# The first layer's token lists: small products over four token tiles at a time, with unlike tiles masked

## The chip, the cores and the metric

The kernel runs on one core of one Trainium2 chip. Its time is the device time of one execution in microseconds; the median of the runs is compared. A core has five engines that are told of here by these names: PE (TensorE, matrix products; PEld is its loading of weights), DVE (VectorE), ACT (ScalarE), POOL (GpSimd) and SP (SyncE, which issues most of the DMA transfers).

## The reference

Two layers work on `x` (8 x 256 tokens of 256 values), each with an attention and a feed-forward part. The change lies in the feed-forward part of the first layer. Its tokens are dealt out to 8 experts of 256 tokens each, one expert after the other, and each expert takes the 256 best of those that are left:

```python
def balanced_assignment(scores):            # T = 2048 tokens, E = 8 experts
    C = T // E
    taken = jnp.zeros((T,), dtype=bool)
    parts = []
    for e in range(E):
        s = jnp.where(taken, -jnp.inf, scores[:, e])
        _, idx = jax.lax.top_k(s, C)
        parts.append(idx)
        taken = taken.at[idx].set(True)
    return jnp.concatenate(parts)
...
sort_by_expert = balanced_assignment(scores)
routed = feat[sort_by_expert].reshape(E, C, D)
h = layer_norm(routed, ln_g, ln_b)
h = jax.nn.gelu(jnp.einsum('ecd,edf->ecf', h, w1) + b1[:, None, :])
h = jnp.einsum('ecf,efd->ecd', h, w2) + b2[:, None, :]
out = routed + h                            # put back at the tokens' own places
```

The order of the tokens inside an expert's list does not matter, since each row is put back where it came from.

## The kernel before, in words

**Order.** The order of the instructions on each engine is written out by hand (the part runs under a manual schedule); each engine works through its own queue in that order. `work` is a queue of small pieces of TensorE work with a cost each, mostly 0.43 us: two products with 128x256 f32 results. `fill(us)` (L1179) takes pieces from it until their costs reach the number given. The pieces are first the keys and values of the second layer's attention (`keys`, `vals`, lines L1398 and L1422), later each expert's two matrix products (`up`, L2388, and `down`, L2405).

**Search.** For each of the first seven experts `search` (L2158) finds the score above which the expert's 256 tokens lie, in five rounds. A round counts on VectorE how many scores of each row lie above a threshold (`count`, L2172), sums the counts by a small product on TensorE (`pcn`, L2189, waits for the count), and makes the next threshold on VectorE (L2194, L2199). Between a count and its product the fillers run: 1.29 us of them a round for experts 0, 1 and 2, around 1.73 to 2.58 for the later ones.

**Lists.** `list_tokens` (L2216) turns the threshold into the list of the expert's tokens, in steps. For experts 0 and 1 all steps run between two searches, with fillers between; for experts 2 to 5 one step is put into each round of the next search; the last two lists run side by side after the last search, with 1.29 us of fillers between steps. The 2048 tokens stand as 16 tiles of 128. The steps are:

1. `sel` marks the chosen tokens (L2227, L2231), and `pse` (L2236) turns the marks into columns.
2. `ppl` (L2262, L2263) gives each token its place in the list; a token that is not chosen gets a place out of range. `place` splits into `place >> 4` and `place & 15`. `oab` (L2270) holds the two as one-hot rows of 16 in f16, and `ob` (L2274) is the second one times the token's number.
3. `pid` (L2278): for each of the 16 tiles, a 128x16 block of `oab` (the weights) times the 128x16 block of `ob`, all summed in one 16x16 block of PSUM. The entry (a, b) is the number of the token at place 16a + b. `ids16` (L2282) is its copy in f16.
4. `pix` (L2286): two products with the constant `rowsel` spread the 16 rows over 128 partitions, so that partition p of half r holds row (128r + p) // 16. `m` (L2290) masks away all but column p mod 16 with `bsel`, `idf` (L2292) sums what is left, and `ids` (L2294) holds the numbers as integers.
5. POOL gathers the rows of the list from DRAM by two indirect transfers (L2297) into `R`, and `hand_over` puts the expert up for its products.

**After the list.** `ffn` (L2332) puts two more pieces into `work`: `norm_rows` (ACT, L2342, waits for the gathered rows) and `turn_rows` (TensorE transposes `prt`, L2369, then ACT writes `RT`, L2373), and then the expert's products. `Y` (L2414) is scattered to DRAM by POOL (L2415). The weights of expert e + 2 are loaded (`load_later`, by SP) once those of expert e are used up.

**Set-up.** `rowsel` is built on POOL between 24 and 27 us (L1649 to L1662): a fill, two selects that leave a band, and a cast to f16. POOL's next result is the root for `cs` (L1751), which is first read at `bnd` (L1862).

Of the kernel before, what the change touches and what calls it, by code (L numbers as in the profile page):

```python
# [9 lines left out]
F32 = mybir.dt.float32  # L10
# [4 lines left out]
ALU = mybir.AluOpType  # L15
# [4 lines left out]
P = 128  # L20
# [1066 lines left out]
def fast_path(  # L1087
# [33 lines left out]
    nc = tc.nc  # L1121
    B, S, D = x.shape
    T = B * S
    NT = T // P
# [6 lines left out]
    NCT = CAP // P  # L1131
# [7 lines left out]
    F16 = mybir.dt.float16  # L1139
# [121 lines left out]
    pr = l0.enter_context(tc.tile_pool(name="pr", bufs=1))  # L1261
    pm = l0.enter_context(tc.tile_pool(name="pm", bufs=2))
    ac = l0.enter_context(ExitStack())
    pa = ac.enter_context(tc.tile_pool(name="pa", bufs=1))
    acp = l0.enter_context(ExitStack())
    ps_t = acp.enter_context(tc.tile_pool(name="ps_t", bufs=4, space=PSUM))
# [30 lines left out]
    for dst, src, i in (  # L1297
# [12 lines left out]
        out=bqd.rearrange("o (b c) -> (o b) c", b=B),  # L1310
        in_=L0_xattn_bq.partition_broadcast(B),
    )
    nc.scalar.dma_start(
        out=WZ[:, :, DH : 2 * DH],
        in_=L0_xattn_Wq.rearrange("(kc p) c -> p kc c", p=P),
# [181 lines left out]
    bsel = pr.tile([P, NCT, 16], F32, name="bsel")  # L1497
# [88 lines left out]
    for h in range(TPB):  # L1586
# [4 lines left out]
            start=True,  # L1591
            stop=True,
# [11 lines left out]
        pattern=[[1, 32]],  # L1604
        base=1,
        channel_multiplier=0,
# [16 lines left out]
        out=tri,  # L1623
        in_=tri,
        pattern=[[1, P]],
        compare_op=ALU.is_gt,
        fill=0.0,
        base=0,
        channel_multiplier=-1,
    )  # L1630

    iab = pr.tile([P, NT, 2, 16], I32, name="iab")
    for j, base in enumerate((BASE // 16, 0)):
        nc.gpsimd.iota(
            iab[:, :, j, :],
            pattern=[[0, NT], [1, 16]],
            base=base,
            channel_multiplier=0,
        )
    tok = pr.tile([P, NT, 16], F16, name="tok")  # L1640
    nc.gpsimd.iota(
        tok,
        pattern=[[P, NT], [0, 16]],
        base=0,
        channel_multiplier=1,
        allow_small_or_imprecise_dtypes=True,
    )

    rows_f = pa.tile([16, NCT, P], F32, name="rows_f")  # L1649
    nc.gpsimd.memset(rows_f, 1.0)  # L1650
    for sign, base in ((1, 1), (-1, 16)):
        nc.gpsimd.affine_select(
            out=rows_f,
            in_=rows_f,
            pattern=[[sign * P, NCT], [sign, P]],
            compare_op=ALU.is_gt,
            fill=0.0,
            base=base,
            channel_multiplier=-sign * 16,
        )  # L1660
    rowsel = pr.tile([16, NCT, P], F16, name="rowsel")
    nc.gpsimd.tensor_copy(rowsel, rows_f)  # L1662
    cc.close()

    for kc in range(KC):
# [10 lines left out]
    for tt in range(2):  # L1676
# [4 lines left out]
            start=True,  # L1681
# [534 lines left out]
    def list_tokens(e, then):  # L2216

        if e == E - 1:

            sel = pm.tile([P, TB], BF16, tag="sel", name="sel")  # L2220
            nc.vector.tensor_scalar(
                sel, taken[e - 1], -1.0, 1.0, ALU.mult, ALU.add
            )
        else:
            n, thr = low[e]
            taken.append(pm.tile([P, TB], BF16, tag="taken", name="taken"))
            nc.vector.tensor_scalar(taken[e], n, thr, None, ALU.is_gt)  # L2227
            sel = taken[e]
            if e:
                sel = pm.tile([P, TB], BF16, tag="sel", name="sel")  # L2230
                nc.vector.tensor_tensor(sel, taken[e], taken[e - 1], ALU.subtract)  # L2231
        yield

        pse = ps_t.tile([P, 4, 4], F32, tag="pt", name="pse")
        for j in range(4):
            nc.tensor.matmul(  # L2236
                pse[:, j, :], sel[:, j * P : (j + 1) * P], first, start=True, stop=True
            )
        selt = pm.tile([P, NT], BF16, tag="selt", name="selt")
        nc.vector.tensor_scalar(  # L2240
            selt.rearrange("p (g j) -> p j g", j=4),
            pse,
            1.0,
            None,
            ALU.mult,
            ALU.add,
            accum_out=cnts[:, e : e + 1],
        )
        before = pm.tile([P, NT], BF16, tag="before", name="before")
        nc.vector.memset(before[:, 0:1], 0.0)  # L2250
        nc.vector.tensor_tensor_scan(
            before[:, 1:],
            onesb[:, 0 : NT - 1],
            selt[:, 0 : NT - 1],
            0.0,
            ALU.mult,
            ALU.add,
        )
        yield

        ppl = ps_t.tile([P, NT], F32, tag="pt", name="ppl")
        nc.tensor.matmul(ppl, tri, selt, start=True, stop=False)  # L2262
        nc.tensor.matmul(ppl, onesb, before, start=False, stop=True)  # L2263
        place = pm.tile([P, NT], I32, tag="place", name="place")
        nc.vector.tensor_copy(place, ppl)
        ab = pm.tile([P, NT, 2], I32, tag="ab", name="ab")
        nc.vector.tensor_scalar(ab[:, :, 0], place, 4, None, ALU.logical_shift_right)
        nc.vector.tensor_scalar(ab[:, :, 1], place, 15, None, ALU.bitwise_and)
        oab = pm.tile([P, NT, 2, 16], F16, tag="oab", name="oab")
        nc.vector.tensor_tensor(  # L2270
            oab, ab.unsqueeze(3).to_broadcast([P, NT, 2, 16]), iab, ALU.is_equal
        )
        ob = pm.tile([P, NT, 16], F16, tag="ob", name="ob")
        nc.vector.tensor_tensor(ob, oab[:, :, 1, :], tok, ALU.mult)  # L2274
        yield
        pid = ps_t.tile([16, 16], F32, tag="pt", name="pid")
        for c in range(NT):
            nc.tensor.matmul(  # L2278
                pid, oab[:, c, 0, :], ob[:, c, :], start=(c == 0), stop=(c == NT - 1)
            )  # L2280
        ids16 = pm.tile([16, 16], F16, tag="ids16", name="ids16")
        nc.vector.tensor_copy(ids16, pid)  # L2282
        yield
        pix = ps_t.tile([P, NCT, 16], F32, tag="pt", name="pix")
        for r in range(NCT):
            nc.tensor.matmul(  # L2286
                pix[:, r, :], rowsel[:, r, :], ids16, start=True, stop=True
            )
        m = pm.tile([P, NCT, 16], F32, tag="m", name="m")
        nc.vector.tensor_tensor(m, pix, bsel, ALU.mult)  # L2290
        idf = pm.tile([P, NCT], F32, tag="idf", name="idf")
        nc.vector.tensor_reduce(idf, m, AX.X, ALU.add)  # L2292
        ids = pm.tile([P, NCT], U32, tag="ids", name="ids", bufs=4)
        nc.vector.tensor_copy(ids, idf)  # L2294
        R = pf.tile([P, NCT, D + 2], F32, tag="R", name="R")
        for r in range(NCT):
            nc.gpsimd.indirect_dma_start(  # L2297
                out=R[:, r, :],
                out_offset=None,
                in_=NMd,  # L2300
                in_offset=bass.IndirectOffsetOnAxis(ap=ids[:, r : r + 1], axis=0),
            )
        then(e, ids, R)
        if e == E - 1:
            for r in range(NCT):
                nc.vector.tensor_scalar(
                    at0[:, r, :], row0, idf[:, r : r + 1], None, ALU.is_equal
                )
# [974 lines left out]
    class Up(Unit):  # L3283
        n = TB
# [733 lines left out]
```

## Time and profile before

| | |
|---|---|
| median of 3 runs | 796.91 us (796.48 to 799.59) |
| the profiled execution | 797.35 us |
| its span | 795.6 us |
| granted TensorE clock, mean | 0.995 |
| DMA over the span | 110.88 MB, mean 139 GB/s |

The span runs from the first to the last recorded instruction of the profiled execution; the remaining 1.75 us lie around it. A row of a timeline gives start, length, engine, line, operation, output and inputs with their shapes, and in square brackets how long the engine stood idle before and what ended it. Rows of like instructions in a row are merged ("x16"): the length then runs from the start of the first to the end of the last. Ends of products are modelled, so that two products of 0.17 us may start 0.03 us apart. A row of a tile gives count, the shortest, middle and longest duration in ns, and when the first and last started.

### The profile page before, as it was taken

How to read it: one execution, taken by the hardware profiler on the slowest of the kernel's cores; microseconds unless marked ns; L12 is line 12 of the kernel's file. 1: busy time of each engine (PE TensorE's matmuls, PEld its weight loads, DVE VectorE, ACT ScalarE, POOL GpSimd, SP SyncE). 2: the span in 40 equal slices, each digit the busy share in tenths (PEclk: the TensorE clock that was granted, in tenths of full speed). 3: DMA queues.
4: the chain of work that ended last, by engine and by line, in shares of the span. 5: the costliest groups of instructions: out<-in, count | busy, mean ns of one | idle time of the engine just before them, and what ended most of it. 6: DMA issues, size and time to landing. Idle time of an engine off the chain costs nothing. (4 is left out here: it accounts for less than half of the span.)

```text
span 795.6 us, 13571 instructions
## 1 busy us (share of the span) xinstructions
PE 778.4 (98%) x5008; PEld 617.2 (78%) x5008; DVE 523.1 (66%) x1477; ACT 367.3 (46%) x678; POOL 218.8 (28%) x293
## 2 busy tenths in 40 slices
PE   7999999999999989999999999999999999999997
PEld 6547778888755544548898988898989899999986
DVE  6367887650377886556948595758575959686732
ACT  3334455333378987331416354535353545443330
POOL 6334123131126646533330001111122311203030
PEclk9999999999999999999999999999999999999999
DMA  8294666498261111251114676797659554311023
GB/s 265 74 310 79 223 198 188 160 284 240 71 182 34 28 28 41 65 189 69 42 46 111 197 228 199 173 318 200 190 117 314 104 185 115 98 14 21 8 28 136
DMA packets 110163, 110.88 MB, mean 139 GB/s; under 512 B 31848, under 2 KB 100680, under 8 KB 110056
## 3 DMA queue, kind: packets, MB, share of 16 engines
q1 hardware_dynamic: 101416, 96.61, 40.8%
q0 software_dynamic: 7920, 13.02, 7.9%
q8 instruction: 41, 0.67, 0.4%
q10 hardware_dynamic: 752, 0.30, 0.1%
q14 instruction: 34, 0.28, 0.1%
HBM read 80.61 MB, written 25.37 MB: 133 GB/s over the span
## 5 line engine op out<-in xcount | busy, mean ns | idle before, releaser
L3609 POOL DMA_INDIRECT Od<-Y,ids x32 | 53.2, 1662 | 279.0 <-DVE Y L3421 163.9
L3281 ACT COPY B<-a 128x512 f32<-128x512 f32 (+1 forms) x54 | 28.7, 531 | 166.8 <-PE a L3293 110.4
L2679 ACT ACTIVATE ex<-p,scale 128x1024 f32<-128x1024 f32 x64 | 67.7, 1111 | 16.8 <-PE p L2671 16.8
L3293 PE MATMUL a<-T,HP 128*128 128x256 f32 x288 | 73.9, 379 | 0.0
L3293 PE MATMUL a<-RT,wab 128*128 128x256 f32 x256 | 66.3, 381 | 0.0
L3143 DVE TENSOR_TENSOR cc<-e,s 128x512 f32<-128x512 f32 x44 | 30.4, 690 | 54.1 <-PE e L3293 54.1
L3143 DVE TENSOR_TENSOR act<-act 128x256 f32<-128x256 f32 (+1 forms) x120 | 61.4, 512 | 2.7
L2388 PE MATMUL ph<-RT,w 128*128 128x256 f32 x256 | 62.0, 390 | 0.0
L2405 PE MATMUL py<-w,A 128*128 128x256 f32 x256 | 61.6, 387 | 0.0
L3293 PEld LDWEIGHTS a<-T,HP 128*128 128x128 f32 x288 | 54.0, 190 | 7.0
L3293 PEld LDWEIGHTS a<-RT,wab 128*128 128x128 f32 x256 | 46.6, 190 | 7.3 <-issue 1.6
L2388 PEld LDWEIGHTS ph<-RT,w 128*128 128x128 f32 x256 | 45.1, 190 | 8.0 <-ACT RT L2373 0.5
L2928 POOL DMA_INDIRECT Td<-HP,to x32 | 33.8, 1056 | 62.7 <-DMA Td<-HP,to 55.3
L2405 PEld LDWEIGHTS py<-w,A 128*128 128x128 f32 x256 | 46.3, 190 | 6.1
L2397 ACT ACTIVATE A<-ph,b1c 128x256 f32<-128x256 f32 x64 | 30.3, 473 | 43.8 <-PE ph L2388 39.6
L3143 DVE TENSOR_TENSOR act<-act,cc 128x512 f32<-128x512 f32 x44 | 30.3, 689 | 13.6 <-ACT act L3327 13.3
L2671 PE MATMUL p<-QM,KT 32*128 32x512 f32 x256 | 37.9, 644 | 1.1 <-ACT ex L2679 0.8
L2415 POOL DMA_INDIRECT Yd<-Y,ids x16 | 15.8, 987 | 75.7 <-DVE Y L2414 22.5
L3308 ACT COPY s<-a 128x512 f32<-128x512 f32 x44 | 25.8, 585 | 20.0 <-PE a L3293 20.0
L2688 PE MATMUL pv<-ex,VA 128*32 128x256 f32 x512 | 32.2, 394 | 2.3 <-DVE run L2902 1.5
L3293 PE MATMUL B<-RT,wab 128*128 128x256 f32 x128 | 32.9, 379 | 0.0
L3293 PE MATMUL e<-RT,HP 128*128 128x256 f32 x128 | 32.8, 379 | 0.0
(526 smaller groups left out, 1712.0 us busy)
## 6 DMA issues: line engine op xcount, KB each, us to landing
w<-in_L_ffn_w_dram SPq DMA_DIRECT2D x16, 1024.0 KB, 6.4
wab<-in_L_ffn_w_e_dram SPq DMA_DIRECT2D x16, 1024.0 KB, 8.6
wc<-in_L_ffn_w_e_dram SPq DMA_DIRECT2D x8, 1024.0 KB
sab<-in_L_ffn_w_e_dram SPq DMA_DIRECT2D x32, 256.0 KB, 5.8
R<-Td SPq DMA_DIRECT2D x8, 530.0 KB, 8.2
sc<-in_L_ffn_w_e_dram SPq DMA_DIRECT2D x16, 256.0 KB, 4.2
Td<-blank SPq DMA_DIRECT2D x2, 1590.0 KB
X<-in_x_dram SPq DMA_DIRECT2D x4, 512.0 KB
```

Of the source, the lines that this page charges most:

```text
L2388: nc.tensor.matmul(ph, w1[:, kc, f * P : (f + 1) * P], RT[:, kc, :], start=(kc == 0), stop=(kc == KC - 1),)
L2397: nc.scalar.activation(A[:, f, :], ph, AF.Gelu_apprx_tanh, bias=b1c[:, e, f : f + 1])
L2405: nc.tensor.matmul(py, A[:, f, r * P : (r + 1) * P], w2[:, f, :], start=(f == 0), stop=(f == NF - 1),)
L2671: nc.tensor.matmul(ps[g // 2][:, g % 2].rearrange("p m q -> p (m q)"), KT[rows, c, k0 : k0 + P], QM[b][rows, c].rearrange("p m q -> p (m q)"),
L2679: nc.scalar.activation(e4[:, 2 * j : 2 * j + 2], ps[j], AF.Exp, scale=scale)
L2688: nc.tensor.matmul(pvs[b, c][32 * g : 32 * g + 32, m, :], VA[:, b * TPB + kt, 8 * c + 2 * g + m, :], ex[b, c, kt][:, g, m, :], start=(kt = ...
L2928: nc.gpsimd.indirect_dma_start(out=Td, out_offset=bass.IndirectOffsetOnAxis(ap=to[g][:, k, j : j + 1], axis=0), in_=HP[:, GT * g + j, :], ...
L3143: eng.tensor_tensor(out, a, b, op)
L3281: nc.scalar.copy(self.b[:, 0 : self.n], self.a[:, 0 : self.n])
L3293: nc.tensor.matmul(ps[:, m * HT2 : (m + 1) * HT2], self.w.get(m, left, self.k), self.x.part[right], start=start and m == 0, stop=True, ski ...
L3308: nc.scalar.copy(self.s2, self.a)
L3609: nc.gpsimd.indirect_dma_start(out=Od, out_offset=bass.IndirectOffsetOnAxis(ap=ids, axis=0), in_=Y, in_offset=None, compute_op=ALU.add,)
```

## The change

Four token tiles are taken together (`BL = 4`). The one-hot block of four tiles is a weight of 128x64, and `ob` of the same four tiles a moving operand of 128x64, so that `pid` becomes 64x64 and needs four products in place of sixteen. Of its 4 x 4 blocks of 16x16 only those on the diagonal pair a tile with itself; the copy to `ids16` becomes a product with the mask `like`, which is 1 on the diagonal blocks and 0 elsewhere. The four diagonal blocks are not yet added up: `rowsel` gets 64 rows, so that `pix` adds the four rows that belong to one place group, and leaves 64 columns; `m` is four times as wide, and the sum `idf` runs over all 64 columns. `oab` is laid out with the two one-hot rows apart (2, tiles, 16), so that four tiles lie side by side. `rowsel` and `like` are built once on POOL at the start.

```diff
-    rows_f = pa.tile([16, NCT, P], F32, name="rows_f")
-    nc.gpsimd.memset(rows_f, 1.0)
-    for sign, base in ((1, 1), (-1, 16)):
+    BL = 4
+    rows_f = pa.tile([16 * BL, 16, NCT * P // 16], F32, name="rows_f")
+    nc.gpsimd.memset(rows_f, 0.0)
+    for i in range(BL):
         nc.gpsimd.affine_select(
             out=rows_f,
             in_=rows_f,
-            pattern=[[sign * P, NCT], [sign, P]],
-            compare_op=ALU.is_gt,
+            pattern=[[-1, 16], [0, NCT * P // 16]],
+            compare_op=ALU.not_equal,
+            fill=1.0,
+            base=-16 * i,
+            channel_multiplier=1,
+        )
+    rowsel = pr.tile([16 * BL, NCT, P], F16, name="rowsel")
+    nc.gpsimd.tensor_copy(
+        rowsel.rearrange("a r p -> a (r p)"), rows_f.rearrange("a n b -> a (n b)")
+    )
+    like = pr.tile([16 * BL, BL, 16], F32, name="like")
+    nc.gpsimd.memset(like, 1.0)
+    for sign, base in ((1, 0), (-1, 15)):
+        nc.gpsimd.affine_select(
+            out=like,
+            in_=like,
+            pattern=[[-16 * sign, BL], [0, 16]],
+            compare_op=ALU.is_ge,
             fill=0.0,
             base=base,
-            channel_multiplier=-sign * 16,
-        )
-    rowsel = pr.tile([16, NCT, P], F16, name="rowsel")
-    nc.gpsimd.tensor_copy(rowsel, rows_f)
+            channel_multiplier=sign,
+        )
...
-        oab = pm.tile([P, NT, 2, 16], F16, tag="oab", name="oab")
+        oab = pm.tile([P, 2, NT, 16], F16, tag="oab", name="oab")
         nc.vector.tensor_tensor(
-            oab, ab.unsqueeze(3).to_broadcast([P, NT, 2, 16]), iab, ALU.is_equal
+            oab,
+            ab.rearrange("p n t -> p t n").unsqueeze(3).to_broadcast([P, 2, NT, 16]),
+            iab.rearrange("p n t w -> p t n w"),
+            ALU.is_equal,
         )
         ob = pm.tile([P, NT, 16], F16, tag="ob", name="ob")
-        nc.vector.tensor_tensor(ob, oab[:, :, 1, :], tok, ALU.mult)
+        nc.vector.tensor_tensor(ob, oab[:, 1], tok, ALU.mult)
         yield
-        pid = ps_t.tile([16, 16], F32, tag="pt", name="pid")
-        for c in range(NT):
+        pid = ps_t.tile([16 * BL, 16 * BL], F32, tag="pt", name="pid")
+        for c in range(0, NT, BL):
             nc.tensor.matmul(
-                pid, oab[:, c, 0, :], ob[:, c, :], start=(c == 0), stop=(c == NT - 1)
-            )
-        ids16 = pm.tile([16, 16], F16, tag="ids16", name="ids16")
-        nc.vector.tensor_copy(ids16, pid)
+                pid,
+                oab[:, 0, c : c + BL, :].rearrange("p n w -> p (n w)"),
+                ob[:, c : c + BL, :].rearrange("p n w -> p (n w)"),
+                start=(c == 0),
+                stop=(c == NT - BL),
+            )
+        ids16 = pm.tile([16 * BL, 16 * BL], F16, tag="ids16", name="ids16")
+        nc.vector.tensor_tensor(
+            ids16, pid, like.rearrange("a n w -> a (n w)"), ALU.mult
+        )
         yield
-        pix = ps_t.tile([P, NCT, 16], F32, tag="pt", name="pix")
+        pix = ps_t.tile([P, NCT, 16 * BL], F32, tag="pt", name="pix")
         for r in range(NCT):
             nc.tensor.matmul(
                 pix[:, r, :], rowsel[:, r, :], ids16, start=True, stop=True
             )
-        m = pm.tile([P, NCT, 16], F32, tag="m", name="m")
-        nc.vector.tensor_tensor(m, pix, bsel, ALU.mult)
+        m = pm.tile([P, NCT, 16 * BL], F32, tag="m", name="m")
+        nc.vector.tensor_tensor(
+            m.rearrange("p r (n w) -> p (r n) w", w=16),
+            pix.rearrange("p r (n w) -> p (r n) w", w=16),
+            bsel[:, 0:1, :].to_broadcast([P, NCT * BL, 16]),
+            ALU.mult,
+        )
```

## The prediction

> **What bounds the kernel now.** I read the page first, then the busy time of the engines in stretches of 20 us, then the waits of TensorE's weight loads in the stretch the change touches (58 to 215 us), then the rows of the tile `pid` and the timeline of two lists. The chain of waits helps little: it is followed back for 0.4 us of the end only. Busy times of the page and of four stretches (columns: stretch, length, then busy us and instructions of PE, PEld, DVE, ACT, POOL, then granted clock, DMA share, GB/s):
>
> ```profile
> PE 778.4 (98%) x5008; PEld 617.2 (78%) x5008; DVE 523.1 (66%) x1477; ACT 367.3 (46%) x678; POOL 218.8 (28%) x293
> ```
>
> ```profile
> 60.00:80.00 20.00, 19.95 (x114) 14.87 (x113) 15.56 (x73) 9.58 (x23) 7.78 (x14) 1.00 0.39 80
> 80.00:100.00 20.00, 19.91 (x115) 14.47 (x114) 16.56 (x75) 9.55 (x21) 3.16 (x3) 1.00 0.66 221
> 100.00:120.00 20.00, 20.00 (x132) 15.52 (x130) 16.34 (x76) 10.36 (x22) 5.43 (x5) 1.00 0.69 207
> ...
> 160.00:180.00 20.00, 19.80 (x124) 16.28 (x124) 9.48 (x32) 7.00 (x15) 6.81 (x7) 1.00 0.97 274
> ```
>
> The eight lists are made between 68 and 167 us, where TensorE is busy throughout. A busy TensorE may still be waiting inside a modelled end, so the next view is who the weight loads waited for (waiter, releaser: us in total, times, longest):
>
> ```profile
> PEld L2189 <- DVE above L2172: 4.7, 14, 0.4
> ...
> PEld prt L2369 <- ACT R L2342: 1.0, 4, 0.4
> ```
>
> L2189 is the small product of a search round. Of its 35 loads VectorE's count releases 14, and in the timeline all lie before 100 us. There a round takes 1.53 us, though its six filling products hold TensorE for only 1.30 us (0.216 each, from the 30 in a row at 188.60: (6.64 - 0.38) / 29): VectorE's chain sets the pace. After 100 us no count is late, and TensorE sets it. The list's own rows, and list 3 in the timeline:
>
> ```profile
> L2278 PEld LDWEIGHTS <-oab x128: 85/87/89, 70.5 to 162.4; 128*16 128x16 f16 x128
> L2278 PE MATMUL pid<-ob,oab x128: 169/169/177, 70.5 to 162.5; 128*16 128x16 f16 x128
> L2282 DVE CAST ids<-pid x8: 152/158/164, 71.1 to 162.7; 16x16 f16<-16x16 f32 x8
> ```
>
> ```profile
> 116.36 0.45 PEld L2278 LDWEIGHTS <-oab 128*16 128x16 f16 x16 [0.33 <-DVE t L2199]
> 116.36 0.56 PE L2278 MATMUL pid<-ob,oab 128*16 128x16 f16 x16
> ...
> 116.83 0.09 DVE L2172 DVE_READ_ACCUMULATOR above<-n,t 128x1 f16 x1
> ...
> 116.84 1.99 PE L2388 MATMUL ph<-RT,w 128*128 128x256 f32 x8
> ...
> 118.46 0.10 PEld L2189 LDWEIGHTS <-cnt 128*128 128x128 f16 x1
> ```
>
> The reader is to see that the sixteen pairs hold TensorE for 0.48 us (116.36 to 116.84), that one product starts about 25 ns after the other ((0.56 - 0.17) / 15), and that the count of this round, ready at 116.92, waits until 118.46 for TensorE.
>
> **The change, part by part.**
>
> *Products for `pid`.* Sixteen pairs of weight load and product become four, each with 64 columns of weights and 64 moving columns in place of 16 and 16. No row has a 64 by 64 f16 pair. From below: `pid` itself runs at 25 ns a pair, and so do the four products for `pse`, with 128 bf16 weight columns and 4 moving ((0.24 - 0.164) / 3). From above: the f32 transposes for `prt`, 128 by 128, start 0.11 us apart ((0.60 - 0.27) / 3). I take 25 ns, since rows on both sides of it in weight columns have that. Twelve pairs fewer are then 12 x 25 = 0.30 us a list; at 0.11 us a pair it would be 0.06. The 0.33 us ahead of the first load stay.
>
> [...]
>
> *Products for `pix`.* Two as before, with 64 moving columns for 16 and 64 rows of weights for 16. Between nothing and half of the f32 transposes' spacing, 2 x 0.03 = 0.06 us; I take nothing, by the same rows.
>
> *VectorE.* `ids16` becomes a product with the mask on 64x64, `m` grows from 128x32 to 128x128, and the sum over it likewise. `m` now takes 0.188 us at 32 elements, and `Y` (L2414), also from PSUM, 0.42 at 256: 1.04 ns an element. So `ids16` goes from 0.158 to 0.22 (+0.06), `m` to 0.29 (+0.10). The sum goes from 0.186 by the slope to `kmax` (0.62 at 512) to 0.27 (+0.09). Together +0.25 us a list. From above, 256-element cost for `ids16` and `m`, 512-element cost for the sum: +0.93. `oab` keeps its 512 elements (0.69 us) and only its order changes, and `ob` reads it without gaps: no cost, at most 0.04 gained by the 0.43 us of `sel` at 512.
>
> After 100 us this hides: in list 3 `ids` is done at 120.79 and VectorE's next step waits for TensorE until 121.92. In list 2 it just fits (`ids` done at 106.59, next step at 106.86). The 0.06 of `ids16` lies beside the filler between `pid` and `pix`. What is not covered is `pix` to `ids`, +0.19, for lists 0 and 1 and for the gathers.
>
> *POOL, 24 to 28 us.* Two more selects on `rows_f` (0.43 each), and `like` with a fill and two selects (0.8 to 1.2 by the rows of `tri` and `rows_f`): +1.6 to 2.0 us. POOL stands idle for 1.55 us there, until 27.85. The result that it then makes is first read at 36.05 (`bnd`), and POOL's next task after 29 us starts at 48.16. Cost nothing; without that cover at most 0.5 us. No queue of SP or POOL is passed by, and the list's gathers stay behind `ids`.
>
> **The sum.**
>
> Lists 0 and 1 (VectorE's pace): the chain runs through `pid`, `pix` and `ids` to the next search, so -0.30 + 0.19 = -0.11, and I take -0.1 each. In list 0 the next step (`n`, 72.67) starts 0.23 us late with no releaser shown, and may gain nothing.
>
> List 2: TensorE comes 0.30 earlier to the load at 104.24, but the count is done at 104.06, and a load follows its count by 0.05 (66.22 to 66.27), so 0.13 is allowed; together -0.33. Its gather then goes out with `ids`, +0.19 against TensorE, and its rows are what `prt` at 113.24 to 113.87 waits for (its four products spread over 0.52 us instead of 0.33). That leaves -0.15.
>
> Lists 3 to 7: full, 5 x -0.30 = -1.5; together -1.65.
>
> List 6's rows: `prt` at 174.03 waits 0.43 us for them. The gathers of 165.71 and 166.98 land only near 172.6, behind the transfers issued from 157.4 on (DMA 0.97 busy). These move only by what is gained by 157, about 1.05, so some 0.4 is lost there. Sum -1.65 + 0.4, about **-1.2 us**.
>
> After 167 us nothing of the change is left, and every later stage is bound by TensorE or follows it, so I carry the gain to the end. The profiled execution took 797.35 us (span 795.6): 796.15. It stands 0.44 above the median of the runs, 796.91, so on that scale **795.7**.
>
> **The rivals.**
>
> 1. *The wide loads are slow* (53 ns a pair, half the transposes' spacing): 0.22 us a list. Lists 0 to 2 gain nothing (0.22 against 0.19, and the late gather), lists 3 to 7 gain 1.1, list 6 gives back 0.3: -0.8, 796.1. For it: no row has 64 columns. [...]
>
> 2. *The gain goes to a transfer.* The rows of list 6 come at a time that DMA sets and not TensorE, or a later load does the same: 796.9, no change. For it: DMA 0.97 busy and 6.9 us to landing. Against: the transfers ahead are issued when TensorE frees the buffers.
>
> 3. *All of it counts*: gathers follow, and lists 0 to 2 are not held: 8 x 0.30 = 2.4, 794.5. Against: 14 loads released by VectorE.
>
> 4. *Slower: VectorE's longer tail from `pix` to `ids`* lies on the path of lists 0 to 2 and of the gathers of lists 2 and 6. It decides from the point at which 0.38 less three pair times is under the tail's growth: 63 ns a pair with +0.19, sooner if the wide reads of PSUM cost more. At 0.11 us a pair and a growth of 0.6: 3 x 0.54, plus 0.6 for list 6, less 5 x 0.06 for lists 3 to 7, +1.9; at +0.4, 3 x 0.34 + 0.4 - 0.3 = +1.1. I set +1.5: 798.4. Against: slopes of 1 ns an element.
>
> 5. That the change does not do what it says is excluded: the order of instructions shows 4 products for 16 in each list, and the same waits.
>
> **How the numbers follow.** Forecast 0.50 (own range 794.9 to 796.5), rival 1 0.17, rival 2 0.13, rival 3 0.08, rival 4 0.12. From 794.2 to 798.0 lie the first three, rival 3 and the milder part of rival 4: about 0.9, and some 0.8 with the spread of the runs (796.48 to 799.59). A measurement of this kernel tells about 0.5%, 4 us, from no change. No case reaches that; I leave 0.06 on each side for several costs together (all of rival 4's upper ends on every list; a later wait that the shift removes).
>
> **What would show it.** Right: products for `pid` about 25 ns apart and the next load 0.18 us after the first, not 0.48; `m` near 0.29 and the sum near 0.27; the lists' start 0.3 us earlier with each from list 3 on; `prt` of list 6 waiting longer than 0.43. Wrong: pairs over 60 ns apart; counts after 100 us that are waited for; a later stage whose start does not move with TensorE.

## Result and the profile after

Over 22 runs of each the changed kernel takes 794.44 us (791.86 to 797.41), the kernel before 796.47 us (795.10 to 799.59): ratio 0.9975, 95% interval 0.9965 to 0.9986, that is 2.0 us less (1.1 to 2.8). 795.7 us had been forecast, 1.2 us less. The measured median lies between the ends given, 794.2 and 798.0, but below the forecast's own range of 794.9 to 796.5, and the terms of the sum are not all what was measured. The profiled execution has a span of 791.2 us and a mean granted clock of 0.998.

The page's line of busy times, then two stretches of 20 us (columns as in the prediction), all of the changed kernel:

```profile
PE 774.4 (98%) x4912; PEld 614.0 (78%) x4912; DVE 525.3 (66%) x1477; ACT 367.7 (46%) x678; POOL 218.5 (28%) x298
```

```profile
80.00:100.00 20.00, 19.91 (x106) 14.46 (x105) 17.00 (x75) 9.54 (x20) 3.16 (x3) 1.00 0.67 216
100.00:120.00 20.00, 19.96 (x107) 15.30 (x106) 16.50 (x77) 10.40 (x22) 5.25 (x5) 1.00 0.70 203
```

TensorE has 96 products fewer, VectorE as many instructions with 2.2 us more work, POOL five more. The waits of weight loads in the stretch 58 to 215 us come next: VectorE's count now releases 16 loads of the search rounds, 14 before, and one of the two new ones is list 2's, at 103.0 (0.17 us). Then the tiles' rows:

```profile
PEld L2205 <- DVE above L2188: 5.3, 16, 0.4
...
PEld prt L2399 <- ACT R L2372: 0.7, 3, 0.3
```

```profile
L2297 PE MATMUL pid<-ob,oab x32: 196/196/217, 69.6 to 160.1; 128*64 128x64 f16 x32
L2305 DVE TENSOR_TENSOR ids<-pid,like x8: 206/210/216, 70.0 to 160.3; 64x64 f16<-64x64 f32 x8
L2315 DVE TENSOR_TENSOR m<-pix,bsel x8: 284/289/292, 70.7 to 163.6; 128x128 f32<-128x128 f32 x8
L2322 DVE TENSOR_REDUCE idf<-m x8: 286/286/288, 71.1 to 163.9; 128x2 f32<-128x128 f32 x8
```

List 3 in the timeline of the changed kernel:

```profile
114.12 1.11 PE L2418 MATMUL ph<-RT,w 128*128 128x256 f32 x4
...
115.16 0.20 PEld L2297 LDWEIGHTS <-oab 128*64 128x64 f16 x4 [0.33 <-DVE t L2215]
115.16 0.31 PE L2297 MATMUL pid<-ob,oab 128*64 128x64 f16 x4
115.40 1.59 PEld L2418 LDWEIGHTS ph<-RT,w 128*128 128x128 f32 x8
...
115.52 0.09 DVE L2188 DVE_READ_ACCUMULATOR above<-n,t 128x1 f16 x1
...
117.02 0.10 PEld L2205 LDWEIGHTS <-cnt 128*128 128x128 f16 x1
```

The group now holds TensorE from 115.16 to 115.40, 0.24 us in place of 0.48. Its products start (0.31 - 0.196) / 3 = 38 ns apart. The idle 0.33 us ahead of the group have stayed, and the count, ready at 115.61, still waits for TensorE. From the start of the four filler products ahead of the group to the fillers behind it TensorE takes 1.28 us (114.12 to 115.40); before the change it took 1.52 (115.32 to 116.84). The group for `pix` has the same idle time ahead of it. Two rows of before:

```profile
115.32 1.11 PE L2388 MATMUL ph<-RT,w 128*128 128x256 f32 x4
...
119.74 0.11 PEld L2286 LDWEIGHTS <-rowsel 16*128 16x128 f16 x2 [0.33 <-issue]
```

### The profile page after: what moved, and what is told of

It reads as the page before. It is cut to its first block, busy times and chain, and to the rows that moved or that the text cites. A ratio compares the mean times of both kernels' runs of the same rounds, so it can differ in the third digit from the quotient of the medians.

```text
span 791.2 us, 13388 instructions
## 1 busy us (share of the span) xinstructions
PE 774.4 (98%) x4912; PEld 614.0 (78%) x4912; DVE 525.3 (66%) x1477; ACT 367.7 (46%) x678; POOL 218.5 (28%) x298
## 5 line engine op out<-in xcount | busy, mean ns | idle before, releaser
L2958 POOL DMA_INDIRECT Td<-HP,to x32 | 32.9, 1028 | 60.4 <-DMA Td<-HP,to 54.9
L3173 DVE TENSOR_TENSOR act<-act,cc 128x512 f32<-128x512 f32 x44 | 30.3, 689 | 13.5 <-ACT act L3357 13.3
L3338 ACT COPY s<-a 128x512 f32<-128x512 f32 x44 | 25.8, 587 | 20.0 <-PE a L3323 20.0
L3173 DVE TENSOR_TENSOR cc<-a,s 128x512 f32<-128x512 f32 x44 | 30.4, 691 | 3.8
```

Of the source, the lines that this page charges most:

```text
L2958: nc.gpsimd.indirect_dma_start(out=Td, out_offset=bass.IndirectOffsetOnAxis(ap=to[g][:, k, j : j + 1], axis=0), in_=HP[:, GT * g + j, :], ...
L3173: eng.tensor_tensor(out, a, b, op)
L3338: nc.scalar.copy(self.s2, self.a)
```

## Where the time went

Four points of each profiled execution are compared: F, the first `few` (the first round of the first search); P, `pbp` (L2975 of before, the first product after the experts of lists 6 and 7); S, `slot_e` (L3658, in the second layer); and the end, where SP has issued the last transfer of the output (the span goes on for 3.9 to 4.8 us until it has landed). F to P holds all lists. All in us; the number of runs behind a time stands in brackets. The four stages are always those of one execution.

| kernel | time | F | F to P | P to S | S to end |
|---|---|---|---|---|---|
| before | 796.47 (22) | 60.37 | 150.25 | 175.01 | 406.00 |
| b_again (before again) | 796.69 (1) | 58.44 | 150.33 | 176.58 | 405.56 |
| changed | 794.44 (22) | 59.52 | 148.53 | 174.27 | 404.69 |
| a_again (changed again) | 792.60 (1) | 58.27 | 149.49 | 174.22 | 404.68 |
| tail_alone | 796.15, ratio 1.0012 (0.9995 to 1.0028) | 58.07 | 150.08 | 174.37 | 406.27 |
| sum_early | 792.25, ratio 0.9958 (0.9943 to 0.9974) | 58.18 | 148.07 | 174.50 | 404.52 |
| setup_alone | 796.29 (1) | 58.60 | 150.28 | 174.80 | 406.09 |
| bl8 | 790.14 (1) | 58.56 | 146.52 | 174.38 | 404.68 |
| bl8_again | 789.76, ratio 0.9943 (0.9929 to 0.9957) | 58.21 | 146.50 | 174.34 | 404.66 |
| sum8 | 791.01, ratio 0.9926 (0.9907 to 0.9945) | 58.72 | 147.77 | 174.46 | 404.51 |
| cols128 | 789.98 (1) | 57.92 | 146.74 | 174.41 | 404.60 |
| rows128 | 790.14 (1) | 58.02 | 147.07 | 174.36 | 404.67 |
| padded | 799.81 (1) | 59.37 | 150.89 | 178.95 | 404.67 |
| padded2 | 797.10 (1) | 59.40 | 148.24 | 178.42 | 405.39 |

The kernel before, run beside them, took 795.22 us for b_again, a_again, tail_alone and sum_early, 796.00 for setup_alone, bl8, sum8 and padded, and 794.32 for cols128, rows128, padded2 and bl8_again; compare times within such a group. F moves between 57.9 and 60.4 whatever the kernel, so its part of a difference is not the change's. Nor do the stages of single executions add up to the difference of the medians: the changed kernel's profiled execution is 4.4 us shorter than that of before, and a_again is 4.1 us shorter than b_again, where the medians differ by 2.0. Both profiled executions of the changed kernel (792.93 and 792.60 us) are faster than its median. How the 2.0 us divide among the stages is therefore not shown; what follows explains the stages.

How much shorter the step of a list is than in the profile of before, by the starts of `few` around it (the last column: from the last search to `kmx`, the maximum behind lists 6 and 7):

| kernel | list 1 | list 2 | list 4 | list 5 | 6 and 7 |
|---|---|---|---|---|---|
| changed | 0.07 | 0.24 | 0.22 | 0.23 | 0.43 |
| a_again | 0.06 | 0.26 | 0.21 | 0.23 | 0.43 |
| tail_alone | -0.17 | 0.00 | -0.02 | -0.02 | -0.04 |
| sum_early | 0.22 | 0.25 | 0.25 | 0.25 | 0.49 |
| cols128 | 0.31 | 0.30 | 0.46 | 0.46 | 0.92 |
| rows128 | 0.17 | 0.44 | 0.43 | 0.43 | 0.87 |
| bl8 | 0.07 | 0.10 | 0.69 | 0.69 | 1.14 |
| sum8 | 0.21 | 0.16 | 0.72 | 0.72 | 1.43 |

These steps repeat within 0.03 us between two executions of one kernel; that is why one execution settles them. The steps of lists 0 and 3 are left out because they do not repeat: list 3's differs by 0.09 between the two executions of before, and padded and padded2, which have the same lists, gain 0.04 and 0.37 there. Two gains are to be explained: 0.22 to 0.26 us a list, and 0.9 to 1.3 us behind S (b_again to a_again, before to changed), where nothing was changed.

## The experiments

**The two kernels again.** 

> The kernel before once more, to see what varies from run to run. Theory: all of the change's gain lies in the list stretch, from the first 'few' of the searches to the product 'pbp' behind the last expert (before: 150.25 us, changed: 148.53). Then this stretch comes out at 150.2 within 0.3, while the start (first 'few' at 60.4 before, 59.5 in the changed kernel) and the part behind 'pbp' (581.0 before, 579.0 changed) may fall anywhere between. Rival: the change moved the start and the later stages too; then the first 'few' is again at 60.4 within 0.1 and the part behind at 581.0 within 0.3.

> The changed kernel once more. Theory: list stretch 148.5 within 0.3; start and the part behind 'pbp' vary as in the kernel before and overlap with it. Rival: first 'few' again at 59.5 within 0.1 and the part behind again at 579.0 within 0.3.

Measured: b_again's stretch came out as expected (150.33), a_again's did not (149.49 for 148.5 within 0.3). The part behind P, 578.9, repeated within 0.1 in a_again, as its rival had it; b_again's, 582.1, fits neither. The steps of the table repeat; list 0 does not. In a_again its step lost 0.80 us against before where the first profile of the changed kernel gained 0.14. What VectorE waits for there is the score row of the next search, a DMA transfer. It cost 1.35 us in sum8 and 1.80 in padded. A row of sum8's timeline; the same step had idled 0.23 us in before:

```profile
72.49 0.75 DVE L2180 SCALAR_TENSOR_TENSOR n<-n,lo,row 128x512 f32<-128x512 f32 x1 [1.87 <-DMA row<-SCd]
```

An early F is not the reason: cols128 has the earliest F (57.92) and gains 0.38 in list 0, padded has one of the latest (59.37) and loses most. SP issued the first transfer of these rows at 63.4 us in cols128 and at 67.4 us in padded; why that varies was not settled.

**tail_alone: the longer VectorE steps without the fewer products.**

```diff
-        ids16 = pm.tile([16, 16], F16, tag="ids16", name="ids16")
-        nc.vector.tensor_copy(ids16, pid)
+        ids16 = pm.tile([16, 16 * BL], F16, tag="ids16", name="ids16")
+        nc.vector.tensor_tensor(
+            ids16.rearrange("a (n w) -> a n w", w=16),
+            pid.unsqueeze(1).to_broadcast([16, BL, 16]),
+            only,
+            ALU.mult,
+        )
...
```

The mask `only` is 1 in its first block of 16 and 0 elsewhere. The sixteen products stay; `pix`, `m` and the sum are as in the changed kernel.

> The sixteen products of the kernel before, with VectorE's wide steps of the changed one: the copy to ids16 is 64 wide (three of four blocks set to nothing by a mask), pix, m and the sum have 64 columns. Theory: the tail from pix to ids grows by 0.2 us (m 0.29 for 0.19, sum 0.29 for 0.19); this costs in lists 0 and 1 in full, in list 2 by what its next step waits (0.1 to 0.2), at the rows of list 2 and of list 6 up to 0.2, and nothing in lists 3 to 7: list stretch 150.25 + 0.5 to 0.8 = 150.8 to 151.1, ratio about 1.001. Rival: VectorE's 0.26 us counts in every list: 152.3, ratio 1.0026. Second rival: hidden everywhere: 150.25.

List 1 pays 0.17 (0.19 had been worked out for `pix` to `ids`), lists 4 to 7 pay 0.02 each. The tail is hidden wherever TensorE sets the pace, as forecast. The stretch, 150.08, missed the 150.8 to 151.1 that were expected and lies nearest to the rival "hidden everywhere": list 2 paid nothing, list 0 only 0.10.

**sum_early: the products of the change, with the diagonal blocks added up ahead of `pix`.**

```diff
...
-            ids16, pid, like.rearrange("a n w -> a (n w)"), ALU.mult
-        )
+            own, pid.rearrange("a (n w) -> a n w", w=16), like, ALU.mult
+        )
+        with nc.allow_low_precision(reason="one term of each sum is not 0"):
+            nc.vector.tensor_reduce(
+                ids16, own.rearrange("a n w -> a w n"), AX.X, ALU.add
+            )
...
```

`pix`, `m` and the sum `idf` are as before, the new step lies beside the fillers between `pid` and `pix`.

> The changed kernel with the sum over the four blocks moved ahead of pix: a reduction of the masked 64x64 to 64x16 on VectorE (0.2 to 0.25 us) behind the mask product, and pix, m and the last sum 16 wide as in the kernel before. Theory: the reduction lies beside the filler between pid and pix, the tail behind pix is 0.2 shorter: lists 0 and 1 gain 0.2 each against the changed kernel, the rows of list 2 come 0.1 to 0.2 earlier, lists 3 to 7 stay: list stretch 148.5 - 0.4 to 0.6 = 147.9 to 148.1, ratio to the kernel before 0.997. Rival: VectorE's tail did not limit lists 0 to 2: 148.5 as in the changed kernel. Second rival: the filler is too short for mask and reduction, and pix waits in lists 0 and 1: 148.5 to 148.8.

Lists 1, 2 and 4 to 7 now all gain 0.22 to 0.25: list 1 gets back the 0.15 that the tail took. It beats the changed kernel by 0.46 us in F to P.

**setup_alone: POOL's new set-up with the lists of before.**

> The kernel before with the new set-up on POOL alone: rows_f, rowsel and like are built as in the change (like is not used), the lists are those of before. Theory of the prediction (the set-up is hidden in POOL's idle time): stretch of the lists 150.1 to 150.4 us as before, first few at 58 to 60.5 us as in the other runs. Rival (the set-up delays the start): first few later than 60.5 us. Slot_e to the end: 405.6 to 406.3 us if the later gain belongs to the products that were taken away, 404.5 to 404.7 if it comes from the set-up.

F at 58.60, F to P 150.28, S to end 406.09: no cost, and no gain behind S. The set-up is hidden.

**bl8: `BL = 8`, two pairs of 128x128.**

> The changed kernel with eight tiles at a time: two pairs of 128x128 per list in place of four of 64x64. If a pair's price followed the weight columns and 128 of them were loaded as fast as in pse (25 ns), the next product would start 0.15 us after the group; if the price grows with the columns from 25 ns at 16 and 38 ns at 64 to about 55 to 65 ns at 128, 0.18 to 0.19. So lists 3 to 7 gain 0.05 to 0.09 us each. VectorE's tail grows: ids16 to 0.28, m to 0.42, the sum to 0.39 to 0.42; from pix to ids 0.24 more than with four tiles, which lists 0 and 1, list 2 and the gathers pay for. Stretch of the lists 148.7 to 149.3 us where the changed kernel has 148.5 (first few near 59.5) and 149.5 (first few near 58.3): so 0 to 0.5 us longer at the same start.

The theory behind this expectation fell. The stretch came out at 146.5, not 148.7 to 149.3, though VectorE's tail grew as foreseen (`m` 0.42, the sum 0.42). Lists 4 and 5 gain 0.69 us where 0.3 was the most that the pair price allowed. What is gone is the idle 0.33 us, ahead of `pid` and ahead of `pix`. List 3 in its timeline:

```profile
113.75 0.31 PEld L2297 LDWEIGHTS <-oab 128*128 128x128 f16 x2
...
116.62 0.31 PEld L2311 LDWEIGHTS <-rowsel 128*128 128x128 f16 x2
```

Either the loads are now wide enough to run beside the product ahead of them, or it hangs on the number of products. Two kernels tell that apart.

**cols128: four products still, but each load takes 128 columns.**

```diff
-        pid = ps_t.tile([16 * BL, 16 * BL], F32, tag="pt", name="pid")
+        pid = ps_t.tile([P, 16 * BL], F32, tag="pt", name="pid")
+        wide = oab.rearrange("p t n w -> p (t n) w")
...
-                oab[:, 0, c : c + BL, :].rearrange("p n w -> p (n w)"),
+                wide[:, c : c + 8, :].rearrange("p n w -> p (n w)"),
...
-            ids16, pid, like.rearrange("a n w -> a (n w)"), ALU.mult
+            ids16, pid[0 : 16 * BL], like.rearrange("a n w -> a (n w)"), ALU.mult
```

> The changed kernel with one thing changed: each of the four weight loads for pid takes 128 columns (its own four tiles and the next four) in place of 64; the rows of pid that belong to the next four are not read. Still four products, the moving side stays at 64 columns, pix is as in the changed kernel. Theory F (a load of all 128 rows and 128 columns runs beside the product ahead of it, any narrower one waits 0.33 us for that product to end): no idle time of 0.33 us ahead of the group for pid, and the filler behind pid starts 1.10 to 1.20 us after the start of the four filler products ahead of it (1.28 in the changed kernel, 1.52 before, 1.05 with eight tiles): 0.08 to 0.18 us a list gained in lists 3 to 7, 0.15 to 0.35 over lists 6 and 7. Theory N (the idle time hangs on the number of products or on the moving side): the idle 0.33 us stay and nothing is gained, or up to 0.06 us a list are lost through the wider loads. The group for pix keeps its 0.33 us and its 1.20 us by both.

List 3 in its timeline:

```profile
112.06 1.11 PE L2419 MATMUL ph<-RT,w 128*128 128x256 f32 x4
...
112.80 0.37 PEld L2298 LDWEIGHTS <-oab 128*128 128x128 f16 x4
113.01 0.28 PE L2298 MATMUL pid<-ob,oab 128*128 128x64 f16 x4
...
113.13 1.97 PE L2419 MATMUL ph<-RT,w 128*128 128x256 f32 x8
...
114.96 1.11 PE L2419 MATMUL ph<-RT,w 128*128 128x256 f32 x4
...
116.00 0.11 PEld L2312 LDWEIGHTS <-rowsel 64*128 64x128 f16 x2 [0.33 <-issue]
```

The load starts at 112.80, 0.21 us ahead of its product and beside the filler products, without a wait; the fillers go on 1.07 us after the start of the four ahead (1.28 in the changed kernel). The products start (0.28 - 0.193) / 3 = 29 ns apart, closer than the 38 ns of half as many weight columns. `pix` has 64 rows of weights and keeps its 0.33. The gain of 0.24 us a list over the changed kernel is above the 0.08 to 0.18 expected.

**rows128: `rowsel` and `ids16` with 64 more rows of zeros.**

```diff
-    rows_f = pa.tile([16 * BL, 16, NCT * P // 16], F32, name="rows_f")
+    rows_f = pa.tile([P, 16, NCT * P // 16], F32, name="rows_f")
...
-    rowsel = pr.tile([16 * BL, NCT, P], F16, name="rowsel")
+    rowsel = pr.tile([P, NCT, P], F16, name="rowsel")
...
+    idz = pr.tile([P, 2, 16 * BL], F16, name="idz")
+    nc.gpsimd.memset(idz, 0.0)
...
-        ids16 = pm.tile([16 * BL, 16 * BL], F16, tag="ids16", name="ids16")
+        ids16 = idz[:, e % 2]
...
-            ids16, pid, like.rearrange("a n w -> a (n w)"), ALU.mult
+            ids16[0 : 16 * BL], pid, like.rearrange("a n w -> a (n w)"), ALU.mult
```

> The changed kernel with one thing changed: rowsel and ids16 have 128 rows in place of 64, the further ones zero, so that pix's two weight loads are 128 by 128; the moving side stays at 64 columns and pid is as in the changed kernel. Theory F: no idle time of 0.33 us ahead of the group for pix, and the filler behind it starts about 1.03 to 1.06 us after the start of the four filler products ahead (1.20 in the changed kernel): 0.13 to 0.18 us a list gained in lists 3 to 7, 0.26 to 0.36 over lists 6 and 7. Theory N: the idle time stays and nothing moves. The group for pid keeps its 0.33 us and its 1.28 us by both. ids16 on VectorE as in the changed kernel, 0.21.

```profile
113.02 0.20 PEld L2299 LDWEIGHTS <-oab 128*64 128x64 f16 x4 [0.33 <-DVE t L2217]
...
115.12 1.11 PE L2420 MATMUL ph<-RT,w 128*128 128x256 f32 x4
115.85 0.31 PEld L2313 LDWEIGHTS <-rowsel 128*128 128x128 f16 x2
116.07 0.22 PE L2313 MATMUL pix<-idz,rowsel 128*128 128x64 f16 x2
...
116.12 0.46 PE L2420 MATMUL ph<-RT,w 128*128 128x256 f32 x1
```

The mirror image: `pid`, 64 columns, waits 0.33; `pix`, 128 rows, does not, and takes 1.00 us from filler to filler in place of 1.20. Adding rows of zeros gains 0.21 us a list, above the 0.13 to 0.18 expected. With the 0.22 of the changed kernel and the 0.24 of cols128 that makes 0.67, close to bl8's 0.69. Theory F holds in both: with all 128 rows and all 128 columns the load starts 0.21 and 0.22 us ahead of its product, with fewer of either it comes 0.33 us late. These runs show which loads start early, for f16 loads behind f32 products; for what reason, no run shows.

**sum8: sum_early with eight tiles; bl8_again: bl8 timed.**

> The version with the diagonal blocks added up ahead of pix (sum_early), with eight tiles at a time: two pairs of 128x128, then own at 128x128 (0.28) and its sum to 16 columns (0.29), both beside the fillers between pid and pix in lists 2 to 7; pix, m and the sum as before the change. Theory: 0.05 to 0.09 us a list gained against sum_early in lists 3 to 7, lists 0 and 1 lose up to 0.1 each: stretch of the lists 147.6 to 148.1 us against 148.07, ratio to before 0.995 to 0.996. Rival (the two longer steps on VectorE make counts late again): stretch over 148.3, ratio 0.997 or more.

> The kernel with eight tiles at a time again, for an interval. By its first look (790.1 us, a stretch of the lists of 146.5 us, 3.7 us less than before, and 1.3 us less from slot_e on) about 5 us under the kernel before: ratio 0.991 to 0.995. If the first look was a lucky one, above 0.996. Lists 4 and 5 should again gain 0.69 us each against before, 0.44 to 0.47 against the changed kernel.

sum8's stretch, 147.77, falls into its range for the wrong reason: lists 4 to 7 gain 0.72 each and list 0 loses 1.35 to the row shown above. Its ratio, 0.9926, is below the 0.995 to 0.996 expected. bl8_again repeats bl8. Against the kernel before, the changed one gains 2.0 us, bl8 4.5 (0.57% of 794.32) and sum8 5.9 (0.74% of 796.00; 5.0 between the medians). The intervals of the two overlap, so which is the better is open; sum8's stretch has the 1.35 us of list 0 in it. cols128 and rows128 together, with VectorE's short tail, were not run.

**padded and padded2: the gain behind S.** Without these two, twelve executions fall into two kinds there: 405.56 to 406.27 in the four with 16 products a list, 404.51 to 404.69 in the eight with fewer. The chain behind it is: of the 32 scatters of `Td` (POOL, L2928) 27 wait, by the trace, for the landing of the one ahead; the last one releases a load `R` from `Td`; VectorE's read of `R` stands in its queue ahead of a step (`X`, L3375) that frees the PSUM tile `a` for TensorE (419.67 and 419.82 in before). In before TensorE waits there, in the changed kernel it does not. In b_again, tail_alone, setup_alone and padded2 all products up to this wait stand as far behind S as in the changed kernel, within 0.03 us; 55 us behind S they are 0.70 to 1.58 us late, and that stays to the end. A row of before:

```profile
420.29 1.13 PE L3293 MATMUL a<-HT,wab_-1_2724 128*128 128x256 f32 x4 [1.15 <-DVE X L3375]
```

The scatters of before, then those of the changed kernel at the same place:

```profile
359.93 0.97 POOL L2928 DMA_INDIRECT Td<-HP,to  x1 [1.80 <-DMA Td<-HP,to]
365.38 1.22 POOL L2928 DMA_INDIRECT Td<-HP,to  x1 [4.48 <-DVE T L3143]
```

```profile
357.68 0.97 POOL L2958 DMA_INDIRECT Td<-HP,to  x1 [2.01 <-DMA Td<-HP,to]
360.98 0.97 POOL L2958 DMA_INDIRECT Td<-HP,to  x1 [2.33 <-DVE ts L2943]
```

One scatter comes 5.45 us after the other in before, 3.30 in the changed kernel. VectorE is named as the releaser in both and is not it: the indices of these scatters (`to`, L2915) were done by 348.8 us in before. The DMA view of before from 358 to 367 us (40 slices of 0.225 us) shows what else ran:

```profile
GB/s 0 0 0 415 189 0 0 0 0 0 0 0 0 0 0 264 302 0 0 73 0 0 0 19 0 19 0 0 0 0 0 0 0 0 0 0 0 0 0 0
...
q8 instruction: 1, 0.02, 0.7%
```

The scatter's packets go out in the slices from 361.4; in slice 20 a 16 KB packet of instructions starts (73 GB/s for 0.225 us), and two late packets follow it in the slices from 363.2 and 363.6. In the four executions with 16 products queue q8 has such a packet 22.9 to 23.7 us ahead of `rows_u` (the step just ahead of S), where the one scatter is late, and 5.7 to 6.7 us behind it, where another is; in the changed kernel its packets lie elsewhere (33.1 and 0.8 us ahead, 21.0 us behind). The theory: 192 TensorE instructions fewer move them (q8 has 41 packets in before, 40 in the changed kernel). The padded kernels put as many small products into the start-up:

```diff
-    for _ in range(12):
+    ones16 = pa.tile([P, 16], F16, name="ones16")
+    nc.vector.memset(ones16, 1.0)
+    for _ in range(6):
         nc.tensor.matmul(pwarm, ones, ones, start=True, stop=True)
+    for _ in range(102):
+        nc.tensor.matmul(pwarm[0:16, 0:16], ones16, ones16, start=True, stop=True)
```

padded2 has 108 in place of 102.

> The changed kernel, with as many small f16 products added to TensorE's start-up as the change took away from the lists (102 weight loads and products of 16x16 in place of 6 of the 12 warm-up products), so that everything behind stands at about the place in TensorE's instructions that it had before the change. The stretch of the lists (first few to pbp) should be as in the changed kernel, 148.3 to 149.6 us by every theory. From slot_e to the end the kernels with 16 products took 405.6 to 406.3 us, those with 4 took 404.5 to 404.7. Theory A (the 1.3 us come from where the later instructions stand): 405.6 to 406.3, with the gap between the 16th and the 17th scatter of Td near 5 us again. Theory B (they come from the lists being earlier): 404.5 to 404.7 and a gap near 3.3 us. Theory C (chance): either.

> As the padded kernel, with 108 small pairs in place of 102, which makes the number of TensorE's recorded instructions that of before (5008). In the ten kernels so far a 16 KB transfer of instructions (queue q8) lies 23 to 24 us ahead of rows_u and again 5 to 6 us behind it in those with 16 products a list, and nowhere near in the others (21 ahead and 7 behind in the padded kernel). Theory A (such a transfer holds up the scatter of Td whose packets are behind it, the chain of scatters ends later, and TensorE waits for it at the end): the transfers lie at 22 to 24 ahead and 5 to 6.5 behind; if they meet a scatter, the gap from the 16th to the 17th scatter is 4.5 to 5.5 us, the last scatter is issued 30 us or more after rows_u and slot_e to the end takes 405.4 to 406.3 us. Theory B (it is the lists or the products themselves): gap near 3.3 us, last scatter before 29.2 us, 404.5 to 404.7 us.

padded came out at 404.67, which spoke against theory A until its q8 packets were read: 21 us ahead of `rows_u` and 7 behind, and from the 16th scatter on none was late by 2 us. It is six pairs short of the mark, because each of the six warm-up products that it leaves out is recorded as two (24 records for 12 in before; 5002 products in all, 5008 in before). Its stretch, 150.89, missed the 148.3 to 149.6 "by every theory", through list 0. padded2 has the packets at 23.1 ahead and 5.9 behind, where before has them (22.9 and 5.8), with the lists of the changed kernel. Its scatters there:

```profile
360.54 0.97 POOL L2962 DMA_INDIRECT Td<-HP,to  x1 [1.87 <-DMA Td<-HP,to]
365.46 0.97 POOL L2962 DMA_INDIRECT Td<-HP,to  x1 [3.95 <-DVE T L3177]
```

4.92 us apart again, and 405.39 us from S to the end, 0.01 under the range given. POOL's first gather behind the last scatter starts 30.3 us after `rows_u` (30.5 to 31.2 with 16 products, 26.9 to 29.1 otherwise), with a wait of 0.30 us back at TensorE. The 30 us of the expectation belong to this gather; the last scatter itself starts 27.0 us after `rows_u` (27.1 to 27.8 and 23.7 to 25.8). Theory A holds: padded and padded2 have the same lists, and the place of the instruction packets decides.

P to S is some 4 us longer in both padded kernels, and 2.3 longer in b_again than in the changed kernel. The traces show the same thing there, one step further. A row of padded2 and the 8 us behind it (columns as in the prediction), then the same place in the changed kernel:

```profile
314.67 0.33 PE L2655 MATMUL pt<-ident,HP 128*128 128x128 f32 x1 [1.46 <-POOL HP L2631]
...
315.64:323.64 8.00, 7.02 (x29) 4.10 (x33) 1.00 (x4) 2.70 (x3) 3.23 (x4) 0.58 0.14 51
```

```profile
314.01 0.33 PE L2651 MATMUL pt<-ident,HP 128*128 128x128 f32 x1 [0.37 <-POOL HP L2627]
...
314.05:322.05 8.00, 6.39 (x56) 3.70 (x57) 4.34 (x18) 2.71 (x3) 4.15 (x4) 1.00 0.11 37
```

TensorE waits for POOL 1.46 us in padded2, 2.10 in padded and 1.03 in b_again, 0.37 in the changed kernel. POOL is late by its fourth scatter, 4.13 us behind the third in padded2 and 3.03 in the changed kernel; in padded2 a q8 packet starts at 307.5 and lasts 1.4 us, and two of the third scatter's 32 packets of over 2 KB go out only at 308.9 and 309.4, behind it. In all three executions the wait is followed by a granted clock of 0.50 for 3.4 us or more; in the changed kernel the clock stays at 1.00. That this clock belongs to the longer wait rests on these four executions alone; no kernel of its own tested it. b_again is the kernel before, so this stage can differ by 2 us between two executions of one kernel.

## Why the prediction came out close, step by step

- **Pair price.** Taken as 25 ns, measured 38. The saving is 0.24 us a list (0.30 forecast, 0.22 by rival 1). This is the mis-sized term. In the sum lists 2 to 7 have 0.13 - 0.19 + 1.5, about 1.45 (the 1.65 hold lists 0 and 1 too); they gained 1.20 (from list 1's end to `kmx`) against the profile of before and 1.1 against b_again. No run shows the 53 ns of rival 1, half the transposes' spacing by its own words and so an estimate (15 x 0.025 - 3 x 0.053 = 0.22; the 0.38 of rival 4 is the same 15 x 0.025): pairs with 64 weight columns start 38 ns apart, those with 128 (and 64 moving ones too) 29.
- **"The 0.33 us ahead of the first load stay."** True, and the largest cost was passed over with that sentence: the two idle times, ahead of `pid` and ahead of `pix`, together are 0.66 us a list, against the 0.24 that the change won. cols128 and rows128 won 0.24 and 0.21 of it back.
- **VectorE's tail.** +0.05, +0.10, +0.10: 0.25 as forecast, hidden after 100 us, +0.17 in list 1 alone. List 1 gained 0.07 (0.1 forecast); list 0 gained 0.14 in one execution of the changed kernel and lost 0.80 in the other, by the score row.
- **List 2.** The limit of 0.13 was read off the start of a weight load that ran 0.21 ahead of its product; the load can wait and the product still come on time: in the changed kernel it waited 0.17 and ran 0.07 ahead, and the product started 0.96 after the four fillers ahead of it, as in before. The list gained 0.24 where 0.13 was allowed. Its late rows cost about 0.1 and not 0.19 (list 3's step is 0.11 and 0.12 shorter, those of lists 4 and 5 0.22). The net is a gain of about 0.14 where the sum has a loss of 0.06: two errors, in the same direction.
- **List 6's rows, +0.4.** Not there in the two executions of the changed kernel. `prt` of list 6 waits at most 0.14 us in them, and not at all in b_again. From `kmx` to P they stand 0.29 and 0.31 under the profile of before, the other executions with 16 products 0.42: a loss of 0.1. But the wait comes and goes: padded, with the same lists, waits 0.42 and takes as long as before there, padded2 does not wait. So the 0.4 are a cost of some executions, not of the change.
- **POOL's set-up at nothing.** Confirmed by setup_alone.
- **"I carry the gain to the end."** This failed: behind S another 0.9 to 1.3 us came, from where TensorE's instruction packets fall. No step and no rival had it. By size it can account for the 0.8 us between the forecast gain of 1.2 and the measured 2.0, but the stages of the kept executions do not add up to the medians, so that is not shown. The list terms came out smaller than forecast and an unforeseen one was added: that the number came so close is in part luck.
- **Rivals.** Rival 3 names 794.5 us, nearly the median, but its cause (0.30 us on each of eight lists) is not what was measured. Rival 1's 0.22 us a list is nearer to the measured saving than the forecast's 0.30, though its pair price of 53 ns is about as far off as the forecast's 25. Rival 4 did not come: pairs far under 63 ns, slopes of 1 ns an element.

## What to carry to other kernels

Look at the idle time ahead of a group of small products (0.33 us here) before its pairs: filling weights up to 128 rows and 128 columns, with zeros (0.21 us a list) or with unread neighbours (0.24), won as much here as taking three quarters of the products away (0.22). A wait seen in one execution is not yet a term of a sum until a second execution has it. And the changed number of instructions moved a stage that the change does not touch by 0.9 to 1.3 us, so compare by stages before a cause is named.

## What the runs showed that was not expected

- Weight loads of f16 behind f32 products: 128x16, 128x64, 16x128 and 64x128 start 0.33 us late; 128x128 start 0.21 and 0.22 us ahead of their product (cols128, rows128). Spacing of pairs: 25 ns at 16 columns, 38 at 64, 29 at 128 (the last two with 64 moving columns).
- A packet of instructions held up the kernel's own transfer: two of a scatter's 32 packets of over 2 KB started only when the 16 KB packet was over (0.94 us in before, 1.4 in padded2), the scatter behind came 1.1 to 2.2 us late, and by the chain behind it TensorE stood for 0.3 to 1.2 us. q8 moved 0.67 MB in 41 such packets in before. The cost measured here fell on a transfer that POOL issues.
- Steps on VectorE follow their elements closely, at about 1 ns an element: `m` 0.188, 0.289 and 0.42 us at 32, 128 and 256, the sum 0.186, 0.286 and 0.42.
